# Three rotating score banks, moved maxima and a pipelined FFN in a pre-norm attention and FP8 FFN kernel

## The chip, the cores and the metric

The kernel runs on one core of one Trainium2 chip. The metric is the device time of the whole launch in microseconds (us); lower is better. Engines are named as the profile names them: PE is TensorE (matmuls), PEld its weight loads, DVE is VectorE, ACT is ScalarE, POOL is GpSimd, and SP is the queue that issues most DMAs.

## The reference

The input x has 2 batches of 2048 tokens of 512 values. A layer norm, grouped-query attention with 16 query heads and 2 key heads of 32 values, and a residual come first. A second layer norm, an FP8 matmul with one scale for all of x and one for the weight, and a second residual follow.

```python
def _L0_attn_ref(x, wq, bq, wk, bk, wv, bv, wo, bo):
    q = (x @ wq + bq).reshape(b, s, H, hd)          # H = 16, hd = 32
    k = (x @ wk + bk).reshape(b, s, G, hd)          # G = 2
    v = (x @ wv + bv).reshape(b, s, G, hd)
    ...
    q = q * cos + rotate_half(q) * sin
    q = q * hd ** (-0.5)
    k = k * cos + rotate_half(k) * sin
    ...
    scores = jnp.einsum('bqhd,bkhd->bhqk', q, k_exp) * hd ** (-0.5)
    attn = jax.nn.softmax(scores, axis=-1)
    out = jnp.einsum('bhqk,bkhd->bqhd', attn, v_exp).reshape(b, s, d)
    return out @ wo + bo

def _L0_ffn_ref(x, weight):
    w_fp8, w_scale = _quant_e4m3(weight)            # scale = max(|t|) / 448
    x_fp8, x_scale = _quant_e4m3(x2d)               # one scale for all of x
    out2d = _scaled_mm(x_fp8, w_fp8.T, x_scale, w_scale)
    return out2d.reshape(*x.shape[:-1], out2d.shape[-1])
...
x = x + _L0_attn_ref(_layernorm(x, axis=-1), ...)
x = x + _L0_ffn_ref(_layernorm(x, axis=-1), L0_ffn_weight)
```

## The kernel before

Tokens are cut into 8 blocks of 512 (`NBLK`), four to a batch; a block has 4 tiles of 128 rows. Queries are cut into 4 quads of 4 heads, and each quad of a block into 2 halves of 256 queries. One quad half is a unit; there are 64, in order.

**Scores twice.** The softmax needs each row's largest score before the exponential. `scores_for_maxima` computes the scores of the next unit with queries on the partitions: 32 matmuls of 128x512 (L457), each into one PSUM bank of the pool `ps_s`, each reduced by DVE (L464) into `part`. The pool has two banks. They come in pairs: two matmuls and two reductions, then a `yield`. At the end of a unit's scores DVE takes the largest over the key blocks (`mx`, L471), casts it into the first half of `mrow` (L472), and subtracts it to get the second half, the rest that the cast lost (L473). `gather_maxima` transposes `mrow` on PE into one more `ps_s` bank (`mtp`, L484), and ACT copies it out as `mT` (L488). The main pass computes the scores with keys on the partitions: `probabilities` lets PE subtract the maxima (L826, first two chunks only) and accumulate the scores (L835) in one of two double banks `T`, and ACT takes the exponential (L844) into `p`. POOL adds pairs of `p` (L818), DMAs add some of these sums to others (L886, L888), and `columns` multiplies p with the values (L795) and sums with ones (L806), both into the bank `avs`. `finish_heads` copies `avs` out on ACT (L774), takes reciprocals on DVE (L778) and multiplies on POOL (L779).

**The order of the work.** It is written out by hand (`manual_schedule`); each engine runs its own instructions in that order. A unit has 4 rounds of 4 key chunks. A round is: one pair of scores, two T chunks and their exponentials, a pair, in the last round `gather_maxima`, a `fill` on PE (not in round 0), the third T chunk, a pair, the fourth chunk, a `fill` on PE, a pair, two `fill`s on DVE, and `columns`. A unit's last pair of scores stands in round 2 of the unit before it.

**Side work.** Projections, norms and finishing are generators, which `Job` wraps. Each `yield` names the engine that its next piece needs (`ON_PE`, `ON_DVE`, `OTHER`), and `fill` runs one piece of the first job that is able to and due (`job.due <= step[0]`; a step is a round). `queue` holds the jobs that use a projection bank, and only its first job runs: the key and value projection of a block four ahead (`project_kv`), the query projection of the next block (`project_q`), the output projection (`finish_block`), the FFN weight (`prepare_weight`). `beside` holds jobs without such a bank: `stack_keys` (keys and their differences to the keys 256 earlier, `dk`, are split into two halves by ACT and POOL and stored to DRAM), `turn` (rotary embedding of queries) and `second_norm`. In the main loop all projections use one PSUM bank of the pool `ps_work`, through `bank`. Each evacuates it on ACT (`pq`, `pk`, `tp`, `tv`, `wtp`) or on DVE (`po`).

**Norms.** `layernorm_stats` makes mean and variance on DVE and lets POOL take the power that gives `rstd` (L190). `second_norm` then normalizes each tile into a scratch (L524) and takes its largest absolute value (L533), which is all that it is for: the common scale of x for the FFN.

**FFN.** After all units, for each half of a block (2 tiles): ACT scales x (L924), DVE rounds it to FP8 values in four instructions (`round_e4m3`, L210 to L216), PE transposes each tile (L936), ACT copies it (L938), PE multiplies (L941), ACT scales the product (L945), DVE adds the residual (L946), and SP stores the half (L948). Here the order is not written by hand.

Of the kernel before, what the change touches and what calls it, by code (L numbers as in the profile page):

```python
# [16 lines left out]
P = 128  # L17
# [10 lines left out]
def preln_attn_fp8_ffn_kernel(  # L28
# [54 lines left out]
    ON_PE, ON_DVE, OTHER = "PE", "DVE", "other"  # L83
    BACK = HB
# [12 lines left out]
    ps_s = ctx.enter_context(tc.tile_pool(name="ps_s", bufs=2, space=bass.MemoryType.PSUM))  # L97
    ps_av = ctx.enter_context(tc.tile_pool(name="ps_av", bufs=1, space=bass.MemoryType.PSUM))
    ps_work = ctx.enter_context(tc.tile_pool(name="ps_work", bufs=1, space=bass.MemoryType.PSUM))
# [4 lines left out]
    spread = [0]  # L104

    def bank(name, dtype=F32):

        shape = [P, TB * 4 // mybir.dt.size(dtype)] if dtype != F32 else [P, TB]
        if attending[0]:
            return ps_work.tile(shape, dtype, tag="work", name=name)  # L110
        if name[:2] in ("pk", "pq"):
            pool, tag = (ps_av, "av") if name[1] == "k" else (ps_work, "work")
            return pool.tile(shape, dtype, tag=tag, name=name)
        spread[0] += 1
        return ps_t.tile(shape, dtype, tag="EO"[spread[0] % 2], name=name)

# [61 lines left out]
    def layernorm_stats(src, mean, rstd, name, tiles=range(NT)):  # L178
# [11 lines left out]
        nc.gpsimd.tensor_tensor(rstd[:, at], var[:, at], neg_half[:, at], ALU.pow)  # L190

    def quantized_scale(amax, scale, inv, name):
# [4 lines left out]
        nc.vector.tensor_reduce(whole, across[:1, :P], AX.X, ALU.max)  # L197
        down = bank(f"down_{name}")

        nc.tensor.matmul(down[:, :1], sel[:1, 0, :].bitcast(F32), whole, start=True, stop=True)  # L200
        nc.vector.tensor_scalar(scale, down[:, :1], -1.0 / E4M3_MAX, 1e-12, ALU.mult, ALU.max)
        nc.vector.reciprocal(inv, scale)
# [27 lines left out]
    def normalized(n, xt, xnT, name):  # L230
# [17 lines left out]
        for i in range(0, NT, 2):  # L248
# [4 lines left out]
            for h in (i, i + 1):  # L253
# [8 lines left out]
                )  # L262

# [77 lines left out]
    def project_kv(n, xt, xnT, csb):  # L341
# [14 lines left out]
        nc.scalar.activation(kv, pk, AF.Identity, bias=bkv_sb)  # L356
        if attending[0]:
            u = swapped(kv, KD, f"k_{n}")
        else:
            u = yield from rotated(kv, csb, f"k_{n}")  # L360
# [7 lines left out]
        )  # L368
        if attending[0]:
# [4 lines left out]
    def stack_keys(n, kv, u, csb):  # L374
# [6 lines left out]
        for what in ("kS", "dkS"):  # L381
# [3 lines left out]
            else:  # L385
                src = t2(f"dk_{n}")[:KD]
                nc.gpsimd.tensor_tensor(src, kx[:, BACK:], kx[:, :TB], ALU.subtract)
            far = halves_far[what, b]
# [13 lines left out]
    def project_q(n, xnT, csb):  # L402
        q = wide.tile([P, QUADS, TB], F32, tag="q", name=f"q_{n}", bufs=2)
        for m in range(QUADS):
# [5 lines left out]
            nc.scalar.activation(raw, pq, AF.Identity, bias=bq_sb[:, m : m + 1])  # L410
            if attending[0]:
# [34 lines left out]

    def scores_for_maxima():

        for u, (k, half) in enumerate(units):
# [3 lines left out]
            for i, kb in order if u else sorted(order, key=lambda at: at[1]):  # L453
                for j in range(4):
                    s = ps_s.tile([P, TB], F32, tag="s", name=f"s_{u}_{i}_{kb}_{j}")
# [9 lines left out]
                    if j == 1:  # L465
                        yield u
                if (i, kb) == (HT - 1, NKB - 1):
# [4 lines left out]
                    nc.vector.tensor_copy(mview[:, :, :, 0], mx)  # L472
                    nc.vector.tensor_tensor(  # L473
                        mview[:, :, :, 1], mx, mview[:, :, :, 0].bitcast(F32), ALU.subtract
                    )
# [4 lines left out]
    def gather_maxima(u):  # L480

        tp = ps_s.tile([P, TB], F32, tag="s", name=f"mtp_{u}")
# [21 lines left out]
    def add_output(n, xt, attn, i, dims=range(DC)):  # L504
# [9 lines left out]
        nc.vector.tensor_tensor(xt[:, i, :], po, xt[:, i, :], ALU.add)  # L514

    def second_norm(n, xt, tiles=range(NT)):
# [3 lines left out]
        )  # L520
        for i in tiles:
            yield ON_DVE
            t = t2(f"xn2_{n}_{i}")
            nc.vector.tensor_scalar(  # L524
                t,
                xt[:, i, :],
                mean2[:, n, i : i + 1],
                rstd2[:, n, i : i + 1],
                ALU.subtract,
                ALU.mult,  # L530
            )
            yield ON_DVE
            nc.vector.tensor_reduce(  # L533
                amax2[:, n * NT + i : n * NT + i + 1], t, AX.X, ALU.max, apply_absolute_value=True
            )
# [39 lines left out]
    def prepare_weight(w_all):  # L575
# [8 lines left out]
        nc.vector.tensor_reduce(wmax1, wmax, AX.X, ALU.max)  # L584
        inv = const.tile([P, 1], F32, tag="winv", name="winv")
        quantized_scale(wmax1, w_scale, inv, "w")
        for o in range(DC):
# [6 lines left out]
            tp = ps_work.tile([P, DC, P], BF16, tag="work", name=f"wtp_{o}")  # L594
            for c in range(DC):
                nc.tensor.transpose(tp[:, c, :], w[o][:, c * P : (c + 1) * P], ident_bf)
            nc.scalar.copy(wT[:, :, o * P : (o + 1) * P], tp)

# [59 lines left out]
    class Job:  # L658


        def __init__(self, steps, kind=None, due=0):
            self.steps = steps
            self.due = due
            self.kind = kind or next(steps)

        def step(self):
            self.kind = next(self.steps, None)

# [48 lines left out]
    def enqueue(u):  # L717
# [20 lines left out]
        if n > 0 and n - 1 not in x_asked and soon:  # L738
# [177 lines left out]
    for n in range(NBLK):  # L916
        yt = y_near[n]
        for half in range(NT // 2):
            v = ppool.tile([P, 2, D], F32, tag="p", name=f"v8_{n}_{half}")
            magic = ppool.tile([P, 2, D], F32, tag="p", name=f"magic_{n}_{half}")  # L920
            xq = papool.tile([P, 2, D], BF16, tag="pa", name=f"xq_{n}_{half}")
            for h in range(2):
                i = 2 * half + h
                nc.scalar.activation(  # L924
                    v[:, h, :],
                    yt[:, i, :],
                    AF.Identity,
                    bias=plus[:, n, i : i + 1],
                    scale=times[:, n, i : i + 1],
                )  # L930
            run(round_e4m3(xq, v, magic))
            for h in range(2):
                i = 2 * half + h
                tp = ps_s.tile([P, DC, P], BF16, tag="s", name=f"xtp_{n}_{i}")
                for c in range(DC):
                    nc.tensor.transpose(tp[:, c, :], xq[:, h, c * P : (c + 1) * P], ident_bf)  # L936
# [66 lines left out]
```

## Time and profile before

| What | Value |
|---|---|
| median of 3 runs | 2551.72 us (2551.22 to 2552.48) |
| the profiled execution's own time | 2555.82 us |
| its span, first to last instruction | 2554.0 us |
| mean granted PE clock | 0.944 |
| prologue, to the first L826 | 123 us |
| main loop, to the last L774 | 2297 us |
| last output projection, scale, and FFN | 134 us |
| busy: PE, DVE, POOL, ACT | 2292.0, 1824.7, 1573.9, 1196.8 us |

Busy time is a sum over the span; what bounds a stage is read from which wait ends last there. A wait in the profile is the idle time of one engine, put down to what released it. Ends of matmuls are modelled, so distances between starts say more about PE than its busy time does. Line numbers (L457) are those of the kernel before.

### The profile page before, as it was taken

What the parts mean: (1) busy time and instruction counts of PE and PEld (TensorE: products, weight loads), DVE (VectorE), ACT (ScalarE), POOL (GpSimd) and SP (SyncE); (2) the same over time, 40 slices, a digit from 0 to 9 for tenths busy, and PEclk for the clock granted to TensorE, in tenths of its full rate; (3) what the DMA queues carried; (4) which work ended last, traced back from release to release, by engine and by line L of the source; (5) the groups of instructions that cost most, each with busy time, mean ns of one, the idle gap of its engine ahead of it and who ended that gap; (6) DMA issues with size and microseconds to landing.
All of it is one profiled execution on the core that took longest, in us unless ns stands there. A gap on an engine that the chain in (4) does not pass through costs nothing.

```text
span 2554.0 us, 41075 instructions
## 1 busy us (share of the span) xinstructions
PE 2292.0 (90%) x16514; PEld 1301.2 (51%) x16514; DVE 1824.7 (71%) x2836; ACT 1196.8 (47%) x1381; POOL 1573.9 (62%) x975
## 2 busy tenths in 40 slices
PE   5599999999999999999999989998998898989855
PEld 2255555555555555555555545555554554555422
DVE  3577677767786678767777687777777778777476
ACT  2145445544445444544444445544554444445444
POOL 4267676776667667666657666665675666656700
PEclk9699999999999999999999999999999999999956
DMA  7544554544444446354564444543454344544312
GB/s 225 147 83 94 111 121 99 118 112 87 120 104 116 90 88 149 94 131 93 116 142 91 108 106 94 115 83 86 111 104 98 75 106 109 130 103 99 67 50 83
DMA packets 103263, 271.71 MB, mean 106 GB/s; under 512 B 15776, under 2 KB 16416, under 8 KB 99232
## 3 DMA queue, kind: packets, MB, share of 16 engines
q0 software_dynamic: 36864, 134.23, 27.7%
q1 hardware_dynamic: 63792, 133.47, 17.7%
q8 instruction: 129, 2.11, 0.3%
q10 hardware_dynamic: 2416, 1.38, 0.2%
q14 instruction: 62, 0.51, 0.1%
HBM read 83.43 MB, written 42.99 MB: 49 GB/s over the span
## 4 chain that ended last, share of the span: by engine, by line
PE 54%; DVE 29%; POOL 5%; issue 3%; DMA 3%; ACT 3%; SPq 1%; DVEq 0%; POOLq 0%; ACTq 0%
DVE part L464 19%; PE s L457 14%; PE T L835 11%; PE avs L795 9%; PE avs L806 5%; PE po L268 4%; PE pq L268 3%; POOL pa L818 3%; DVE both L778 2%; PE T L826 2%; PE py L941 2%; DVE mrow L472 2%; ACT p L844 1%; PE mtp L484 1%; DVE sw_q L286 1%
## 5 line engine op out<-in xcount | busy, mean ns | idle before, releaser
L464 DVE TENSOR_REDUCE part<-s 128x1 f32<-128x512 f32 x2048 | 1316.1, 685 | 593.9 <-PE s L457 584.1
L818 POOL TENSOR_TENSOR pa<-p,p 128x1024 f32<-128x1024 f32 x448 | 1078.1, 2411 | 497.1 <-ACT p L844 486.2
L844 ACT ACTIVATE p<-T 128x1024 f32<-128x1024 f32 x1024 | 1004.4, 1023 | 807.3 <-PE T L835 789.4
L457 PE MATMUL s<-kS,qst 128*128 128x512 f32 x2048 | 882.8, 483 | 137.8 <-DVE part L464 79.2
L835 PE MATMUL T<-qst,dkS 128*128 128x512 f32 x2048 | 685.9, 432 | 16.1 <-ACT p L844 15.9
L457 PEld LDWEIGHTS s<-kS,qst 128*128 128x128 f32 x2048 | 376.0, 193 | 591.3 <-DVE part L464 417.3
L795 PE MATMUL avs<-p,vX 128*32 128x256 f32 x8192 | 498.9, 384 | 0.0
L835 PEld LDWEIGHTS T<-qst,dkS 128*128 128x128 f32 x2048 | 376.4, 194 | 159.7 <-issue 53.9
L795 PEld LDWEIGHTS avs<-p,vX 128*32 128x32 f32 x8192 | 240.8, 110 | 216.5 <-issue 71.1
L886 POOL DMA_DIRECT2D pa<-pa x192 | 170.1, 886 | 60.9 <-POOL pa L818 58.3
L774 ACT COPY both<-avs 128x512 f32<-128x512 f32 x64 | 37.5, 586 | 253.1 <-PE avs L806 253.1
L223 POOL TENSOR_TENSOR lo_q<-q,hi_q 128x512 fp32r<-128x512 f32 x32 | 41.1, 1284 | 178.4 <-ACT hi_q L222 178.1
L268 PE MATMUL po<-wo_sb,attn 128*128 128x512 f32 x256 | 135.0, 613 | 3.4 <-POOL attn L779 3.4
L268 PE MATMUL pq<-xnT_q,wq_sb 128*128 128x512 f32 x224 | 117.8, 608 | 0.0
L778 DVE RECIPROCAL both<-both 128x128 f32<-128x128 f32 x128 | 112.5, 920 | 6.5 <-ACT both L774 6.5
L806 PE MATMUL avs<-pa,ones 128*32 128x256 f32 x1536 | 106.3, 379 | 3.1 <-POOL pa L818 2.0
L941 PE MATMUL py<-wT,xqT 128*128 128x512 bf16 x128 | 56.6, 593 | 35.3 <-ACT xqT L938 35.3
L826 PEld LDWEIGHTS T<-mT,sel 128*128 128x128 f32 x512 | 78.8, 190 | 11.9 <-issue 0.4
L888 POOL DMA_DIRECT2D pa<-pa x64 | 75.7, 1183 | 11.7 <-DMA pa<-pa 10.2
L826 PE MATMUL T<-mT,sel 128*128 128x256 f32 x512 | 81.7, 282 | 0.0
L472 DVE CAST mrow<-mx 128x8 fp32r<-128x8 f32 x64 | 76.3, 1192 | 2.2
L779 POOL TENSOR_TENSOR attn<-both 128x256 f32<-128x256 f32 x64 | 65.7, 1026 | 6.0 <-DVE both L778 6.0
(115 smaller groups left out, 1212.9 us busy)
## 6 DMA issues: line engine op xcount, KB each, us to landing
pa<-pa POOLq DMA_DIRECT2D x256, 512.0 KB, 4.7
qst<-q_far SPq DMA_DIRECT2D x128, 256.0 KB, 4.2
x_kv<-in_L_attn_x_dram SPq DMA_DIRECT2D x8, 1024.0 KB, 8.0
q_far<-hi_q SPq DMA_DIRECT2D x32, 256.0 KB, 2.0
q_far<-lo_q SPq DMA_DIRECT2D x32, 256.0 KB, 2.0
x_res<-in_L_attn_x_dram SPq DMA_DIRECT2D x8, 1024.0 KB, 6.3
out_dram<-v SPq DMA_DIRECT2D x16, 512.0 KB, 2.8
sw_q<-q SPq DMA_DIRECT2D x240, 32.0 KB, 2.2
```

The lines of the kernel that those rows point to most:

```text
L268: nc.tensor.matmul(dst, lhs(c), rhs(c), start=(c == 0), stop=(c == chunks - 1))
L457: nc.tensor.matmul(s, qst[k][:, j, at : at + P], stacked["kS"][:, group(k), kb * TB : (kb + 1) * TB], start=True, stop=True,)
L464: nc.vector.tensor_reduce(part[:, i, j, kb : kb + 1], s, AX.X, ALU.max)
L472: nc.vector.tensor_copy(mview[:, :, :, 0], mx)
L778: nc.vector.reciprocal(piece, piece)
L795: nc.tensor.matmul(avs[j * HD : (j + 1) * HD, 0, :], vX[batch(k)][:, kc, group(k), :], p[:, j, :], start=(kc == 0), stop=(kc == NTS - 1), ...
L806: nc.tensor.matmul(avs[j * HD : (j + 1) * HD, 1, :], ones, pa[:, j, :], start=False, stop=(chunks[-1] == NTS - 1 and i == len(sums) - 1), ...
L818: nc.gpsimd.tensor_tensor(pa, a, b, ALU.add)
L826: nc.tensor.matmul(T[:, j, :], sel[:, j, :], maxima[u], start=(j % 2 == 0), stop=True, skip_group_check=True,)
L835: nc.tensor.matmul(T[:, j : j + 2, :], stacked["dkS"][:, group(k), kc * P : (kc + 1) * P], qst[k][:, j : j + 2, half * HB : (half + 1) * H ...
L844: nc.scalar.activation(p, T, AF.Exp, scale=SCALE)
L886: nc.gpsimd.dma_start(out=far_sums[r], in_=pair, accum_op=ALU.add)
```

## The change

Six edits go together.

1. The pool `ps_s` gets three banks by name (s0, s1, s2) and `ps_work` is gone. Scores take the three in turn (`s_bank`). A projection takes the one that is next in turn (`bank` sets `lent`), scores then alternate between the other two, and `give_back`, called where the evacuation has been issued, ends the loan.
2. The first half of the maxima is copied by ACT. The subtraction is put off until the next two reductions have been issued (`split_maxima`), or until `gather_maxima`.
3. A new mark `LATER` makes a job due one round later. It stands after POOL's `rstd`, before the halves of keys and of `dk` are split, and before the weight's scale is made.
4. `second_norm` takes the largest and the smallest value of each raw row (two reductions a tile) and normalizes these two at the end with four small instructions and a reduction, where it normalized the whole tile.
5. Loading x for the residual waits, in most cases, until a buffer of x is free.
6. The FFN is ordered by hand: rounding is issued two halves ahead, a tile's transpose one tile ahead of its product. The rounding's scratch moves to another buffer.

```diff
+    S_BANKS = 3
+    s_next = [0]
+    lent = [S_BANKS - 1]
+    def s_bank():
+        if s_next[0] == lent[0]:
+            s_next[0] = (s_next[0] + 1) % S_BANKS
+        tag = f"s{s_next[0]}"
+        s_next[0] = (s_next[0] + 1) % S_BANKS
+        return tag
     def bank(name, dtype=F32):
...
         if attending[0]:
-            return ps_work.tile(shape, dtype, tag="work", name=name)
+            if lent[0] is None:
+                lent[0] = s_next[0]
+            return ps_s.tile(shape, dtype, tag=f"s{lent[0]}", name=name)
...
+    def give_back():
+        if attending[0]:
+            lent[0] = None
...
         nc.gpsimd.tensor_tensor(rstd[:, at], var[:, at], neg_half[:, at], ALU.pow)
+        if attending[0]:
+            yield LATER
...
             raw = q[:, m, :]
             nc.scalar.activation(raw, pq, AF.Identity, bias=bq_sb[:, m : m + 1])
+            give_back()
...
                 nc.gpsimd.tensor_tensor(src, kx[:, BACK:], kx[:, :TB], ALU.subtract)
+            if attending[0]:
+                yield LATER
+                yield OTHER
             far = halves_far[what, b]
...
+    def split_maxima():
+        if split:
+            mview, mx = split.pop()
+            nc.vector.tensor_tensor(
+                mview[:, :, :, 1], mx, mview[:, :, :, 0].bitcast(F32), ALU.subtract
+            )
...
-                    s = ps_s.tile([P, TB], F32, tag="s", name=f"s_{u}_{i}_{kb}_{j}")
+                    s = ps_s.tile([P, TB], F32, tag=s_bank(), name=f"s_{u}_{i}_{kb}_{j}")
...
                     if j == 1:
+                        split_maxima()
                         yield u
...
                     nc.vector.tensor_reduce(mx, part, AX.X, ALU.max)
-                    nc.vector.tensor_copy(mview[:, :, :, 0], mx)
-                    nc.vector.tensor_tensor(
-                        mview[:, :, :, 1], mx, mview[:, :, :, 0].bitcast(F32), ALU.subtract
-                    )
+                    nc.scalar.copy(mview[:, :, :, 0], mx)
+                    split.append((mview, mx))
...
+        ends = small.tile([P, NT, 2], F32, tag="ends", name=f"ends_{n}_{tiles[0]}")
         for i in tiles:
-            yield ON_DVE
-            t = t2(f"xn2_{n}_{i}")
-            nc.vector.tensor_scalar(t, xt[:, i, :], mean2[...], rstd2[...], ALU.subtract, ALU.mult)
-            yield ON_DVE
-            nc.vector.tensor_reduce(amax2[...], t, AX.X, ALU.max, apply_absolute_value=True)
+            for e, op in enumerate((ALU.max, ALU.min)):
+                yield ON_DVE
+                nc.vector.tensor_reduce(ends[:, i, e : e + 1], xt[:, i, :], AX.X, op)
+        at = slice(tiles[0], tiles[-1] + 1)
+        yield ON_DVE
+        for e in range(2):
+            end = ends[:, at, e]
+            nc.vector.tensor_tensor(end, end, mean2[:, n, at], ALU.subtract)
+            nc.vector.tensor_tensor(end, end, rstd2[:, n, at], ALU.mult)
+        nc.vector.tensor_reduce(amax2[...], ends[:, at, :], AX.X, ALU.max, apply_absolute_value=True)
...
         nc.vector.tensor_reduce(wmax1, wmax, AX.X, ALU.max)
+        yield LATER
+        yield ON_PE
         inv = const.tile([P, 1], F32, tag="winv", name="winv")
         quantized_scale(wmax1, w_scale, inv, "w")
...
         def step(self):
             self.kind = next(self.steps, None)
+            if self.kind == LATER:
+                self.due = step[0] + 1
+                self.kind = next(self.steps)
...
-        if n > 0 and n - 1 not in x_asked and soon:
+        free = len(x_taken) < 3 or x_taken[-3] in x_done
+        if n > 0 and n - 1 not in x_asked and soon and (free or len(queue) <= 1):
...
-    for n in range(NBLK):
-        yt = y_near[n]
-        for half in range(NT // 2):
...
+    with tc.manual_schedule():
+        tiles = [(n, i) for n in range(NBLK) for i in range(NT)]
+        AHEAD = 4
+        for n, i in tiles[:AHEAD:2]:
+            round_half(n, i // 2)
+        ready = transposed(0, 0)
+        for at, (n, i) in enumerate(tiles):
+            if i % 2 == 0 and at + AHEAD < len(tiles):
+                m, j = tiles[at + AHEAD]
+                round_half(m, j // 2)
+            ahead = transposed(*tiles[at + 1]) if at + 1 < len(tiles) else None
+            multiplied(n, i, ready)
+            ready = ahead
```

`round_half`, `transposed` and `multiplied` hold the instructions of the FFN's loop body as they were: scaling and rounding of a half; the transposes of a tile with ScalarE's copy; the product, its scaling, the residual and, after a half's second tile, the store.

## The prediction

> **What bounds the kernel now.** I read the page's busy shares and clock row first, then its chain and groups, then the list of waits, then the timeline at the longest holes of TensorE, and windows over units and stages.
>
> ```profile
> PE 2292.0 (90%) x16514; PEld 1301.2 (51%) x16514; DVE 1824.7 (71%) x2836; ACT 1196.8 (47%) x1381; POOL 1573.9 (62%) x975
> PE 54%; DVE 29%; POOL 5%; issue 3%; DMA 3%; ACT 3%; SPq 1%; DVEq 0%; POOLq 0%; ACTq 0%
> L464 DVE TENSOR_REDUCE part<-s 128x1 f32<-128x512 f32 x2048 | 1316.1, 685 | 593.9 <-PE s L457 584.1
> L472 DVE CAST mrow<-mx 128x8 fp32r<-128x8 f32 x64 | 76.3, 1192 | 2.2
> ```
>
> ```profile
> PEld s L457 <- DVE part L464: 417.3, 933, 6.2
> ...
> ACT hi_dkS L222 <- POOL dk L387: 42.3, 8, 7.5
> ...
> DVE xn L524 <- POOL rstd L190: 16.1, 9, 5.1
> ```
>
> TensorE looks 90% busy, but those ends are modelled, so I took starts. Score matmuls follow each other in 0.22 us when nothing holds them. Counting the main stretch (123 to 2420 us) in start-to-start distances, 1788 us is streaming and 508 us is waiting: about 8 us in each of 64 units of 35.5 us (a unit ends where L774 copies `avs`). Half of it stands before a score matmul `s`: there are two score banks, and a pair may only start when VectorE's maximum has freed each. The chain says so too: 29% of it is VectorE, mostly L464.
>
> The worst recurring wait is at the end of each unit's scores:
>
> ```profile
> 1554.18 4.72 POOL L818 TENSOR_TENSOR pa<-p,p 128x1024 f32<-128x1024 f32 x2 [1.14 <-ACT p L844]
> ...
> 1556.84 0.19 DVE L471 TENSOR_REDUCE mx<-part 128x8 f32<-128x32 f32 x1
> 1557.07 1.88 DVE L472 CAST mrow<-mx 128x8 fp32r<-128x8 f32 x1
> ...
> 1558.98 0.17 DVE L473 TENSOR_TENSOR mrow<-mx,mrow 128x8 fp32r<-128x8 f32 x1
> 1559.07 2.56 DVE L464 TENSOR_REDUCE part<-s 128x1 f32<-128x512 f32 x4
> ...
> 1559.80 0.19 PEld L457 LDWEIGHTS s<-kS,qst 128*128 128x128 f32 x1 [0.70 <-DVE part L464]
> ```
>
> An 8-column cast (175 ns at its shortest) takes 1.88 us and ends as POOL's sum ends (1554.18 + 4.72 = 1558.90). The reductions behind it start late, and the scores behind them.
>
> ```profile
> 1488.29 1.68 POOL L190 TENSOR_TENSOR rstd<-var,neg_half 128x4 f32<-128x4 f32 x1
> ...
> 1490.01 2.57 DVE L524 TENSOR_SCALAR xn<-x_res,mean,rstd 128x512 f32<-128x512 f32 x1 [1.76 <-POOL rstd L190]
> 1492.51 1.28 DVE L464 TENSOR_REDUCE part<-s 128x1 f32<-128x512 f32 x2
> 1493.23 0.29 PEld L457 LDWEIGHTS s<-kS,qst 128*128 128x128 f32 x1 [6.20 <-DVE part L464]
> ```
>
> Here VectorE stands on `rstd`, then on the same coupling, and TensorE stands 6 us.
>
> ```profile
> 682.00:688.50 6.50, 4.56 (x41) 2.36 (x40) 6.33 (x12) 2.30 (x3) 3.93 (x3) 1.00 0.99 303
> 688.50:692.00 3.50, 3.31 (x10) 2.44 (x9) 2.03 (x4) 1.40 (x2) 1.50 (x2) 0.51 1.04 222
> ...
> 1464.10:1502.80 38.70, 32.24 (x243) 18.43 (x244) 30.61 (x48) 16.86 (x19) 21.87 (x13) 0.91 0.32 66
> 1536.20:1568.20 32.00, 30.83 (x243) 17.20 (x244) 24.35 (x37) 16.73 (x18) 20.89 (x12) 1.00 0.35 66
> ...
> 2435.40:2554.00 118.60, 70.90 (x256) 27.21 (x256) 81.63 (x96) 60.16 (x96) 0.00 (x0) 0.56 0.19 71
> ```
>
> Columns: length, busy PE, PEld, DVE, ACT, POOL, granted clock. Two things: after a hole the clock falls to half, and in the FFN no engine is full (DVE 81.6 of 118.6).
>
> **The change part by part**, against the profiled span of 2554.0 us. That execution took 2555.82; the runs' median is 2551.72, so I take the sum off the median.
>
> *Maxima on ScalarE.* From the timeline of 62 units, the score pair before `mtp` waits 1.21 us on average, any other pair 0.06. Without four units held by `rstd` (next part) it is 0.90. The cast leaves VectorE and the subtraction L473 goes behind the next two reductions, so of about 1.8 us ahead of these (0.19, 1.19, 0.44) only `mx` (0.19) stays: 62 x (0.90 - 0.06), about 52, take 50. On ScalarE the copy is new; L774 (512 columns, 0.586) and L488 (256, 0.373) give an estimate of 0.17 us, 11 us in all, and before the next exponential ScalarE stands 2.95 us for TensorE at 1559.17. Behind it in ScalarE's queue stand the exponentials, and TensorE's T behind those: if `mx` came over 2 us late they would wait. VectorE can be three reductions late (1.9 us), so cost 0, bound 64 x 0.5 = 32.
>
> *POOL's results a round later.* `dk` holds ScalarE, so the exponentials, so T: holes of 4.08 us at 287, 533, 826 and 1119 us, 3.2 each: 13. `rstd` of the second norm: holes of 6.1 at 1493, 1773, 2135, 2279, less the 1.2 just counted: 19. The weight's largest: one of 4.9 at 1943: 4. `rstd` for keys: 3. Together 39. The two `lo` sums, `dk` and four stores a block move: in the order of instructions the `dkS_far` stores of blocks 5 to 7 go behind eight `sw_q` transfers on SP's queue, `lo_kS` and `dk` behind sums on POOL's. The key fetch reads them, from 1141.7 us on for block 7, and 16 `sw_q` transfers stand behind it on SP. SP waits 961 us at L437 alone, which covers these 0.45 us issues; cost 0, bound 10 once where the stores come late. The guard on loading x changes nothing: both orders force the same four advances.
>
> *Row ends.* Out: 32 L524 (1.105 mean, 0.544 median) = 35.4. In: 32 more reductions like L533 (0.679) = 21.7, and five small operations per block. The Trainium skill speaks against these: GPSIMD Engine Reference, 1. Specifications, says that GpSimd shares its SBUF interfaces with VectorE and contends with instructions in a two-port mode or with two SBUF inputs. Four of the five have two. If each block's group waits a whole sum (2.4), 9 blocks cost 22 us. The trace's nearest row is L473, two small inputs: median 0.176, mean 0.441, longest 2.31. I take that row: 9 x (4 x 0.441 + 0.2) = 18. VectorE gets +4, in units where it is the long one (30.6 of 38.7): -4; bounds +10 and -15.
>
> *Third bank.* Where no projection holds a bank, three rotate. By the changed order 799 of 2071 score and `mtp` tiles of the main loop find three. At just these places TensorE now waits 187 us, of which 39 is counted above: 148. Not all can go. Following one undisturbed round of unit 39 by hand (pairs when the bank freed three tiles ago is free, T when its exponential ends, VectorE 0.645 a reduction), I get 0.9 us less a round, as the third pair meets VectorE's pace; 97 such rounds give 87. But 14 of these 24 units carry norm work on VectorE. I take 58; ends 0 and 110.
>
> *Hand-overs.* A bank given back is often the very next score's. In the changed order 105 score matmuls wait on ScalarE, before 63 (these for `mT`): 42 new ones, behind `pq` (21), `tp`, `tv`, `wtp`. A score directly behind the last `pq` waits for the exponential ahead and L410 (0.68): up to 1.15 us. A VectorE wait would often stand there anyway: I take 0.5 each, -21; ends 0 and -48. The 14 behind `po` come after the 1.9 us of avs: nothing.
>
> *The clock.* 25 stretches in the main loop run at half clock, 116 us. The Trainium skill's TensorE: Matmul & The Clock Gate (HAM oscillation) lets the clock fall for idle gaps over about 3.4 us; by that only the nine holes over 4 us matter, and the maxima's would cost no clock. The trace differs: at 688.5 the clock is halved right after a hole of 2.2 us, at 1016 after 2.5, at 617 after 1.5. So I count the 18 stretches that follow holes removed here, 92 us; less 24 us idle, half is 34 at most. Units also wait on other engines: 17; by the rule 8.
>
> *FFN.* VectorE's own work is 16 x (0.694 + 0.693 + 1.225 + 1.220) + 32 x 0.692 = 83.4. With rounding two halves ahead it need not stand for L945. First inputs 1.6, the last tiles' TensorE and ScalarE 5, the last store 4 as now, 4 of remaining stalls: 98 against 118.6. TensorE at half clock needs 2.4 a tile, 77, just under it. Gain 20; ends 8 (tiles at 3.1 as now) and 26.
>
> Sum: 50 + 39 - 4 + 58 - 21 + 17 + 20 = 159. 2551.7 - 159 = 2393 us.
>
> **The rivals.** *The third bank comes to nothing* (0.20): waits move from banks to ScalarE's exponentials and the DMA sums. For it: rounds are already 7.0 us at 1472 to 1479, with T just behind the exponential; the last `pa` accumulate is issued at 1559.80, lands 4.7 us later, and its columns need it at 1567.09. Against: in that round three pairs still wait. Then 101 remain, with hand-overs at their worst 74: 2450 to 2478.
>
> *Free units reach their floor* (0.13): third bank 110, clock 34: 2551.7 - 228 = 2324, up to 2345. VectorE's 30.6 us in norm units speaks against.
>
> *Hand-overs decide* (0.05, slower): a projection and the scores now share banks on TensorE's one in-order queue. There are 93 loans and 42 returns behind ScalarE. If each stands for three queued reductions (1.94 us), 262 us are lost against 180 gained elsewhere: 2634. It turns the sign from 1.33 us each. Against: each product takes its bank at least one fill before its first matmul, and 23 loans take back the same bank.
>
> **How the numbers follow.** About 0.2% is what a measurement here tells from no change. Main case 0.61 (2345 to 2445), third bank to nothing 0.20, floor 0.13, hand-overs 0.05, a near-cancelling 0.01. Likeliest 2393; 2328 to 2465 leaves out two in ten, at both sides. Faster 0.94, same 0.01, slower 0.05.
>
> **What would show it.** Right: the mrow copy is ScalarE's at about 0.2 us and the pair before `mtp` waits under 0.3; no T hole behind `dk`, no 6 us hole behind `rstd`; half-clock stretches fall to under ten; units 39, 47 and 61 (32.0 now) take 28 to 29.5, units with projections stay near 34; the FFN takes 95 to 102. Wrong: `s` <- ACT waits above 50 us; units 39 and 47 over 31; `avs` <- DMA or POOL growing from 8 to over 40 us; ScalarE standing on `mx`.

## The result, and the profile after

The changed kernel takes 2513.69 us (median of 4 runs, 2507.04 to 2517.14), the kernel before 2551.47 beside it: ratio 0.9849, interval [0.9827, 0.9871]. That is 38 us less. The forecast was 159 less, and its range ended at 2465. The profiled execution took 2512.17 us, with a span of 2510.1. From here on, a line number in a run's view is that of the run's own kernel: the reduction of the scores is L464 before and L502 after.

The page of the changed kernel: busy time of each engine, the chain's shares, the costliest group.

```profile
PE 2220.7 (88%) x16509; PEld 1286.6 (51%) x16514; DVE 1766.0 (70%) x2817; ACT 1207.4 (48%) x1445; POOL 1571.5 (63%) x975
...
PE 38%; DVE 22%; POOL 15%; DMA 11%; issue 7%; ACT 5%; SPq 1%; POOLq 0%; ACTq 0%; DVEq 0%
...
L502 DVE TENSOR_REDUCE part<-s 128x1 f32<-128x512 f32 x2048 | 1299.6, 682 | 643.6 <-PE s L495 637.9
```

TensorE and VectorE have lost weight in the chain (54 to 38%, 29 to 22%), as meant. POOL has gone from 5 to 15% and DMA from 3 to 11%. The forecast had no term for either.

The list of waits (who waits for whom: us in all, times, longest) shows what fell and what came:

```profile
PEld s L495 <- DVE part L502: 264.1, 675, 5.5
PE mtp L522 <- DVE part L502: 54.2, 39, 4.7
PEld avs L859 <- DMA pa<-pa: 40.2, 30, 3.0
PEld s L495 <- ACT q L437: 32.3, 23, 1.7
PE avs L859 <- DMA pa<-pa: 25.7, 28, 2.5
```

The same waits before, for `mtp` and for the ones-matmuls on the DMA:

```profile
PE mtp L484 <- DVE part L464: 11.9, 58, 0.3
PEld avs L806 <- DMA pa<-pa: 2.6, 4, 1.3
PE avs L806 <- DMA pa<-pa: 1.2, 2, 0.8
```

(One wait can stand in two rows, once for the weight load, PEld, and once for the matmul, PE.) The wait for score banks fell from 417 to 264 us. In its place TensorE stands before `mtp`, before the ones-matmuls that sum the probabilities (L859), and, as new waits, behind `pq`'s evacuation.

TensorE's waiting in the main loop, counted as in the prediction (distance from start to start, less the streaming time of the matmul before), is the table all runs are read with. The loop runs here from the first selection matmul to the last copy of `avs`. A pair of scores has a first and a second matmul.

| us of TensorE waiting before | before | after |
|---|---|---|
| first score of the pair ahead of `mtp` | 74.7 | 2.6 |
| other first scores | 93.2 | 78.4 |
| first scores behind an evacuation | -32.3 | 2.9 |
| second scores | 216.5 | 180.9 |
| T | 87.6 | 72.2 |
| `mtp` | 34.0 | 77.1 |
| ones-matmuls | 1.1 | 42.6 |
| everything else | 30.1 | 24.4 |
| all | 504.9 | 481.1 |

(The negative entry only means that the streaming time used for a product, 0.436 us, is too long where a score follows it; differences count.) Scores, the first four rows, had 352 of the 505 us before, more than the half of which the prediction speaks. About 144 us went and 120 came back. The loop's 24 us and the FFN's 26 (118.6 to 92.3) less some 6 us of a longer prologue make the difference of 44 between the spans. The prologue took 123 to 131 us in the runs of this study, also where no edit touches it.

The largest thing that came back is seen in the timeline of unit 35. It took 35.2 us before and 40.4 after (columns: start, us, engine, line, operation):

```profile
1427.22 1.20 POOL L941 DMA_DIRECT2D pa<-pa  x1
1427.46 4.58 DVE L481 TENSOR_TENSOR mrow<-mx,mrow 128x8 fp32r<-128x8 f32 x1
...
1427.79 1.91 POOL L540 TENSOR_TENSOR x_res<-x_res,bo_sb 128x512 f32<-128x512 f32 x1
1429.03 2.97 POOL L871 TENSOR_TENSOR pa<-p,p 128x1024 f32<-128x1024 f32 x1
1431.96 1.27 DVE L502 TENSOR_REDUCE part<-s 128x1 f32<-128x512 f32 x2
...
1432.79 0.66 PE L522 MATMUL mtp<-ident,mrow 128*128 128x128 f32 x2 [4.68 <-DVE part L502]
```

L481 is the subtraction that the change puts off. It has eight columns and a median of 0.165 us. Here it takes 4.58 and ends as the second of two adjoining POOL sums does (1429.03 + 2.97 = 1432.00, the subtraction at 1432.04). The reductions behind it wait, and `mtp` with them. `mtp` has such holes of 4.9 to 5.0 us in units 14, 22, 30, 35, 43, 53 and 57, and these units are each 5 to 6.5 us longer than before. Units 37, 45, 55 and 59, which waited for `rstd`, became 7 to 9 us shorter.

The groups by tile give the same over all 64 units (shortest, median, longest in ns). Cast and subtraction before:

```profile
L472 DVE CAST mrow<-mx x64: 175/1332/2127, 114.6 to 2380.2; 128x8 fp32r<-128x8 f32 x64
L473 DVE TENSOR_TENSOR mrow<-mx,mrow x64: 174/176/2312, 114.8 to 2381.2; 128x8 fp32r<-128x8 f32 x64
```

and after:

```profile
L511 ACT CAST mrow<-mx x64: 203/205/210, 119.6 to 2362.5; 128x8 fp32r<-128x8 f32 x64
L481 DVE TENSOR_TENSOR mrow<-mx,mrow x64: 154/165/4579, 120.8 to 2362.9; 128x8 fp32r<-128x8 f32 x64
```

In the trace of before, 53 of the 64 casts L472 last over 0.3 us, and every one of the 53 ends 0.03 to 0.04 us behind the end of a POOL instruction. Of the subtractions L481 after, 23 are that long, and again all 23 end so; 10 of these lasted through two POOL operations. So the subtraction meets POOL less often than the cast did, but for longer, and at a place where `mtp` needs it next.

The FFN, in the table by windows (length, then busy PE, PEld, DVE, ACT, POOL, clock):

```profile
2417.80:2510.10 92.30, 52.06 (x251) 23.27 (x256) 80.35 (x101) 59.88 (x96) 0.00 (x0) 0.78 0.24 91
```

VectorE is busy for 80 of 92 us, so here the edit did what it says, and a little more than forecast. (This window opens 0.8 us ahead of the first scaling of x, with which the window before opens; from the first scaling it is 91.4 us.)

### The profile page after: what moved, and what is told of

It is laid out like the page before. It is cut to its first block, busy times and chain, and to the rows that moved or that the text cites. A ratio compares the mean times of both kernels' runs of the same rounds, so it can differ in the third digit from the quotient of the medians.

```text
span 2510.1 us, 41080 instructions
## 1 busy us (share of the span) xinstructions
PE 2220.7 (88%) x16509; PEld 1286.6 (51%) x16514; DVE 1766.0 (70%) x2817; ACT 1207.4 (48%) x1445; POOL 1571.5 (63%) x975
## 3 DMA queue, kind: packets, MB, share of 16 engines
q1 hardware_dynamic: 63792, 133.47, 18.1%
## 4 chain that ended last, share of the span: by engine, by line
PE 38%; DVE 22%; POOL 15%; DMA 11%; issue 7%; ACT 5%; SPq 1%; POOLq 0%; ACTq 0%; DVEq 0%
DVE part L502 12%; POOL pa L871 11%; PE s L495 10%; DMA pa<-pa 9%; PE T L888 7%; PE avs L848 7%; ACT p L897 4%; PE po L290 4%; PE avs L859 3%; DVE both L831 3%; PE pq L290 2%; PE T L879 2%; DVE mrow L481 2%; POOL pa L939 1%; POOL q L324 1%
## 5 line engine op out<-in xcount | busy, mean ns | idle before, releaser
L502 DVE TENSOR_REDUCE part<-s 128x1 f32<-128x512 f32 x2048 | 1299.6, 682 | 643.6 <-PE s L495 637.9
L495 PE MATMUL s<-kS,qst 128*128 128x512 f32 x2048 | 828.5, 466 | 101.3 <-DVE part L502 29.5
L495 PEld LDWEIGHTS s<-kS,qst 128*128 128x128 f32 x2048 | 367.9, 191 | 497.2 <-DVE part L502 264.1
L888 PEld LDWEIGHTS T<-qst,dkS 128*128 128x128 f32 x2048 | 369.8, 191 | 157.0 <-issue 53.7
L939 POOL DMA_DIRECT2D pa<-pa x192 | 169.1, 881 | 60.9 <-POOL pa L871 58.3
L290 PE MATMUL po<-wo_sb,attn 128*128 128x512 f32 x256 | 140.1, 634 | 3.4 <-POOL attn L832 3.4
L859 PE MATMUL avs<-pa,ones 128*32 128x256 f32 x1536 | 107.7, 383 | 36.5 <-DMA pa<-pa 25.7
L859 PEld LDWEIGHTS avs<-pa,ones 128*32 128x32 f32 x1536 | 46.3, 110 | 80.9 <-DMA pa<-pa 40.2
L522 PE MATMUL mtp<-ident,mrow 128*128 128x128 f32 x128 | 29.0, 311 | 61.0 <-DVE part L502 54.2
L941 POOL DMA_DIRECT2D pa<-pa x64 | 74.8, 1168 | 11.8 <-DMA pa<-pa 10.2
```

What stands on the lines that cost most here:

```text
L290: nc.tensor.matmul(dst, lhs(c), rhs(c), start=(c == 0), stop=(c == chunks - 1))
L495: nc.tensor.matmul(s, qst[k][:, j, at : at + P], stacked["kS"][:, group(k), kb * TB : (kb + 1) * TB], start=True, stop=True,)
L502: nc.vector.tensor_reduce(part[:, i, j, kb : kb + 1], s, AX.X, ALU.max)
L859: nc.tensor.matmul(avs[j * HD : (j + 1) * HD, 1, :], ones, pa[:, j, :], start=False, stop=(chunks[-1] == NTS - 1 and i == len(sums) - 1), ...
L888: nc.tensor.matmul(T[:, j : j + 2, :], stacked["dkS"][:, group(k), kc * P : (kc + 1) * P], qst[k][:, j : j + 2, half * HB : (half + 1) * H ...
L939: nc.gpsimd.dma_start(out=far_sums[r], in_=pair, accum_op=ALU.add)
```

## The experiments

Three theories were tried against each other. *Port*: the put-off subtraction waits for POOL. *Hand-overs*: the third bank's gain is lost where scores take over a bank that ScalarE must still empty. *Sums*: the sum that POOL's DMA accumulates lands too late for the ones-matmuls.

| run | what | us | ratio to before |
|---|---|---|---|
| after | all edits | 2513.7 | 0.9849 [0.9827, 0.9871] |
| a_split_now | after, subtraction at once | 2492.5 | 0.9761 [0.9729, 0.9794] |
| a_keep_bank | after, banks handed back to projections | 2503.5 | 0.9799 [0.9761, 0.9837] |
| a_no_third | after, scores on two banks | 2504.9 | 0.9808 [0.9771, 0.9845] |
| a_no_lo | after, no subtraction | 2463.6 | 0.9645 [0.9624, 0.9666] |
| a_no_lo_two | the last two together | 2445.2 | 0.9579 [0.9564, 0.9595] |
| a_old_max | after without edit 2 | 2495.5 | 0.9773 [0.9749, 0.9797] |
| a_old_norm | after without edit 4 | 2522.1 | 0.9866 [0.9851, 0.9881] |
| a_near | after, first sum on TensorE | 2446.0 | 0.9567 [0.9549, 0.9585] |
| b_max | before with edit 2 | 2585.9 | 1.0141 [1.0114, 1.0168] |
| b_direct | before, neither cast nor subtraction | 2515.8 | 0.9845 [0.9827, 0.9863] |
| b_later | before with edit 3 | 2541.1 | 0.9956 [0.9938, 0.9975] |
| b_later_guard | before with edits 3 and 5 | 2526.7 | 0.9888 [0.9868, 0.9908] |
| b_ffn | before with edit 6 | 2530.1 | 0.9898 [0.9860, 0.9936] |
| best1 | two banks, no subtraction, first sum on TensorE | 2439.0 | 0.9543 [0.9522, 0.9564] |
| best2 | best1 with the third bank | 2434.4 | 0.9522 [0.9504, 0.9541] |
| best3 | best2 with banks handed back | 2418.3 | 0.9461 [0.9444, 0.9479] |

The kernel before measured between 2551 and 2555 us in the groups of runs, so the ratios are what is compared below; 0.001 is 2.55 us.

**The subtraction at once.** In a_split_now it stands right behind ScalarE's copy.

```diff
                     split.append((mview, mx))
+                    split_maxima()
```

> The changed kernel (2513.7 us), with the subtraction L481 directly behind ScalarE's copy, not behind the next two reductions. Theory 'port' (L481 has two SBUF inputs and now falls where POOL issues its two sums back to back, up to 4.6 us; mtp waits 77 us where it waited 34): at the old place POOL is at the end of one sum, so L481's mean falls from 0.87 to under 0.5 us, mtp's wait to about 35, and the time by 30 to 45 us, to 2470 to 2484. Theory 'hand-overs' or theory 'sums' (other waits hold TensorE anyway): 2500 to 2515, the wait only moves.

Faster than the changed kernel by about 22 us, less than the port theory asked for. The groups by tile of this run tell why:

```profile
L511 ACT CAST mrow<-mx x64: 203/205/208, 117.2 to 2343.3; 128x8 fp32r<-128x8 f32 x64
L481 DVE TENSOR_TENSOR mrow<-mx,mrow x64: 165/1194/2362, 118.5 to 2343.6; 128x8 fp32r<-128x8 f32 x64
```

The median of the subtraction is now 1.19 us. In before the cast had 1.33 and the subtraction behind it 0.18. So moving the cast to ScalarE does not remove the wait: the subtraction inherits it (57 of 64 wait, each to the end of a POOL sum), while the reduction `mx` ahead of it stays at 0.19 us. Before `mtp` 43.6 us of waiting went, but 48 came back on the scores around it. The run's gain shows in the sums' wait, 42.6 to 24.5, and in small items.

**Edit 2 alone.** b_max is the kernel before with nothing but this edit; its two parts are as in the diff above.

> The kernel before with edit 2 alone (copy on ScalarE, subtraction behind the next two reductions). As forecast: 50 us and a few of clock, 2495 to 2502. If the subtraction takes over the wait for POOL that the cast had (port): what is saved ahead of the two reductions is lost in front of mtp, 2535 to 2555.

It is slower than before, by 1.4%, outside both expectations. The groups by tile of b_max:

```profile
L483 ACT CAST mrow<-mx x64: 203/205/208, 121.4 to 2420.6; 128x8 fp32r<-128x8 f32 x64
L453 DVE TENSOR_TENSOR mrow<-mx,mrow x64: 157/165/4560, 121.6 to 2421.1; 128x8 fp32r<-128x8 f32 x64
```

The pair ahead of `mtp` waits 36 us instead of 75, as the edit intends. `mtp` itself waits 85 instead of 34, and the ones-matmuls 17 instead of 1. T, which stands behind the copy in ScalarE's queue, waits only some 4 us longer.

**Edit 2 taken out.** a_old_max makes both halves on VectorE, at once, in the changed kernel.

```diff
-                    nc.scalar.copy(mview[:, :, :, 0], mx)
+                    nc.vector.tensor_copy(mview[:, :, :, 0], mx)
                     split.append((mview, mx))
+                    split_maxima()
```

> The changed kernel without edit 2: VectorE makes both halves of the maxima at once, as before. If edit 2 is a loss in place as it is alone (port, 34 us alone): 2475 to 2500. If it is needed in the changed order, as forecast: slower than the changed kernel, 2535 to 2565.

0.9773 against 0.9849: in place, too, edit 2 costs some 19 us. a_old_max and a_split_now differ only in the engine of the first half, and their intervals overlap (0.9773 and 0.9761). So the copy's move to ScalarE is worth next to nothing, and what costs is that the subtraction is put off.

**No subtraction.** a_no_lo copies the first halves on ScalarE and stops there.

```diff
                     nc.scalar.copy(mview[:, :, :, 0], mx)
-                    split.append((mview, mx))
```

> The changed kernel without the subtraction L481: the second halves of the maxima stay zero, which a softmax does not see but for rounding. Port theory: the wait before mtp falls from 77 us to about 30 and the reductions behind are on time, 45 to 60 us less: 2454 to 2469. If the DMA sums and hand-overs hold the units anyway (sums): 10 to 20 us less, 2494 to 2504.

52 us less (0.9645 against 0.9849), as the port theory said. `mtp` waits 33.2 us instead of 77.1. The ones-matmuls still wait 52.6.

**What there was to be had.** b_direct reduces the maximum straight into `mrow` in the kernel before.

```diff
-                    nc.vector.tensor_reduce(mx, part, AX.X, ALU.max)
-                    nc.vector.tensor_copy(mview[:, :, :, 0], mx)
-                    nc.vector.tensor_tensor(
-                        mview[:, :, :, 1], mx, mview[:, :, :, 0].bitcast(F32), ALU.subtract
-                    )
+                    nc.vector.tensor_reduce(mview[:, :, :, 0], part, AX.X, ALU.max)
```

> The kernel before with one change: the maximum is reduced straight into mrow, so that neither copy nor subtraction is there (the second halves stay zero). Port theory: all of the 0.84 us that the pair before mtp waits over other pairs goes, and part of the 34 us at mtp: 55 to 80 us less, 2472 to 2497. Rival, that the next wait takes its place: 2520 to 2540.

40 us less, between the two expectations. The pair ahead of `mtp` went from 74.7 to 36.2 only. Some 24 of the 36 stand in units 37, 45, 55 and 59, 5.9 us in each, behind `xn`, which waits for `rstd`: they belong to edit 3. The ones-matmuls came up to 14. So of the forecast 50, this way brings some 40 in the kernel before. No operation is left in it that waits for POOL: the reduction into `mrow` takes 0.19 us in all 64 units (0.191 at the longest).

**The third bank taken out.** In a_no_third the loan never ends, so projections keep the third bank as in the kernel before. a_no_lo_two does the same without the subtraction.

```diff
     def give_back():
-        if attending[0]:
-            lent[0] = None
+        return
```

> The changed kernel with the third bank always lent: scores use two banks and projections the third, as before the change; all other edits stay. If the third bank is worth what the forecast had for it net of hand-overs (37 us): 2551. If hand-overs and the sums eat it: 2500 to 2520. If it costs more than it brings: below 2500.

> As a_no_lo, and projections keep the third bank, so that scores have two. If the third bank is worth what was forecast once the subtraction is out of the way: 35 to 58 us slower than a_no_lo. If it gives and takes alike, as in a_no_third: within 10 us of a_no_lo.

Without the subtraction, two banks are faster than three: 0.9579 against 0.9645. With it the difference is 10 us the same way, 0.9808 against 0.9849, but the intervals overlap a little. The waits tell what it gives and takes. From a_no_third to after, first and second scores lose 48 us of waiting and `mtp` 4; scores behind an evacuation gain 35, the ones-matmuls 21, T 4.

**Banks handed back.** a_keep_bank lets a projection take the bank that the last one gave back, if no score was placed in between.

```diff
     def s_bank():
+        back[0] = None
...
-                lent[0] = s_next[0]
+                lent[0] = s_next[0] if back[0] is None else back[0]
...
     def give_back():
         if attending[0]:
+            back[0] = lent[0]
             lent[0] = None
```

> The changed kernel, but a projection that goes on in the same step keeps the bank that it has just given back, so scores do not land on a bank that ScalarE still has to empty. Theory 'hand-overs' (scores behind an evacuation wait 35 us more than before the change): -20 to -35 us, 2479 to 2494. Theory 'port' or 'sums': within 8 us of 2513.7, with the wait of scores on ScalarE gone and found again elsewhere.

The scores behind an evacuation lose 10 of their 35 us, and the run is 13 us faster by the ratios, whose intervals overlap a little: between the two expectations. `mtp` still waits 73.2 us: the subtraction is a loss of its own.

**The sum on TensorE.** a_near does not let POOL's DMA add the first sum onto the second; four more matmuls a unit sum it in round 2, where it is there already.

```diff
-                    sums = []
+                    sums = [far_sums[0]] if r == 2 else []
                     far_sums.append(add_pair(u, chunks[2], *probs[2:]))
                     nc.gpsimd.dma_start(out=far_sums[r], in_=pair, accum_op=ALU.add)
-                if r == 2:
-                    nc.gpsimd.dma_start(out=far_sums[1], in_=far_sums[0], accum_op=ALU.add)
```

> The changed kernel without the DMA accumulate of the first sum onto the second: TensorE sums the first itself one round earlier. Sums theory: the 42.6 us that the ones matmuls wait go, less 14 us for 4 more matmuls a unit: 2480 to 2492. If the late subtraction ends the units anyway (port alone): 2508 to 2518.

72 us less (0.9567 against 0.9849), more than twice what the sums theory gave, although the expectation priced the added matmuls too low. Each counts twice in the trace: L859 has 2048 records where there were 1536, and a unit's eight more take 0.43 us from start to start, about 27 us in all and not 14. The ones-matmuls fall from 42.6 to 4.6, and `mtp` from 77.1 to 41.2. In the list of waits of a_near:

```profile
PE mtp L522 <- DVE part L502: 21.8, 40, 1.4
...
PEld avs L859 <- DMA pa<-pa: 0.4, 1, 0.4
```

The two losses hang together. Issuing the accumulate (L941) takes POOL 1.2 us, in the same place in each unit: between L939 and what follows. Without it POOL's queue is not in arrears when the subtraction comes. This is read from the rows: the run takes away the late sum, POOL's 1.2 us and the DMA's transfer at once, and none takes away one alone. The timeline of a_near at the place of unit 35 shown above:

```profile
1388.64 1.58 POOL L540 TENSOR_TENSOR x_res<-x_res,bo_sb 128x512 f32<-128x512 f32 x1
...
1389.30 0.96 DVE L481 TENSOR_TENSOR mrow<-mx,mrow 128x8 fp32r<-128x8 f32 x1
...
1390.88 2.37 POOL L871 TENSOR_TENSOR pa<-p,p 128x1024 f32<-128x1024 f32 x1 [0.66 <-ACT p L897]
```

POOL stands 0.66 us between the two sums, and the subtraction gets through in that gap after 0.96 us instead of 4.58. Over all units it now waits in 13 cases instead of 23, and through two POOL operations in 2 instead of 10.

**Pieces a round later.** b_later is before with the mark `LATER`; b_later_guard adds edit 5, the guard on loading x.

```diff
+        free = len(x_taken) < 3 or x_taken[-3] in x_done
-        if n > 0 and n - 1 not in x_asked and soon:
+        if n > 0 and n - 1 not in x_asked and soon and (free or len(queue) <= 1):
```

> The kernel before with edit 3 alone (pieces that need POOL a round later). As forecast: 39 us and some 10 of clock, 2502 to 2515. If the holes behind dk and rstd only give way to the next wait: under 15 us, 2537 to 2550.

> The kernel before with edits 3 and 5. If the 16 us hole of unit 19 in b_later came from an early load of x: it goes, and the forecast 39 us are seen, 2508 to 2522. If the guard has no part in it: as b_later, 2536 to 2548.

Edit 3 alone: 11 us. Unit 19 takes 53.9 us in it (41.6 before). There VectorE stands on the late transfer of query pieces, two waits of 18.1 us together. The row of b_later from 810 to 900 us, which has the longer one:

```profile
DVE sw_q L289 <- DMA sw_q<-q: 10.0, 1, 10.0
```

x is loaded at 822.5 us there, and the query pieces behind it on SP's queue go out from 832.0. With the guard x is loaded behind them (839.4), the unit takes 38.9, and the two edits are worth 29 us together. So the guard, which I had put at nothing, belongs to edit 3.

**The FFN and the row ends.** b_ffn is before with edit 6 alone; a_old_norm is after with the whole-tile `second_norm` of before.

> The kernel before (2551.5 us) with the new order of the FFN alone. The changed kernel's FFN took 92.3 us where 118.6 was: if that is the edit's own, 2523 to 2528; if half of it is the clock that the main loop hands over, about 2538.

> The changed kernel without edit 4: the second norm's largest comes from the whole normalized tile again. As forecast for the row ends (4 us gained): 2510 to 2520. If normalized tiles were waiting for POOL more than was counted: slower, 2525 to 2545.

The FFN's order is worth 26 us by the ratio (16 to 36 by its interval; 21 by the medians). The stage itself takes 91.0 us in the trace of b_ffn, as short as after, so its gain is the edit's own; in b_max and b_direct, with the old order, it takes 118.4 and 116.8. The row ends are worth 4, and their intervals overlap.

**The best of it.** best1 reduces straight into `mrow` as b_direct, keeps two banks for scores and sums on TensorE as a_near. best2 puts the third bank on it, best3 hands banks back as a_keep_bank.

> The changed kernel with the maximum reduced straight into mrow (no copy, no subtraction), two banks for scores, and no DMA accumulate of the first sum onto the second: TensorE sums the first itself one round earlier (4 more matmuls a unit). Sums theory: the 25 us of waits before the ones matmuls go, and POOL is 74 us less busy: 2405 to 2430. If other waits end last there: 2435 to 2450, as a_no_lo_two.

> best1 with the third bank shared as in the change. If the DMA sums were where the third bank's gain went: now it shows, 25 to 45 us faster than best1, 2394 to 2414. If the hand-overs eat it (35 us counted against 42 us): within 10 us of best1, 2429 to 2449.

> best2, and a projection takes again the bank that the last one gave back, if no score has been placed since. If hand-overs are the other half of the third bank's price: 10 to 25 us faster than best2. If not: within 5 us of it.

best3 is faster than both kernels: 2418.3 us, 0.9461. best1 came out at its second expectation, that other waits end last. Against after, no subtraction brought 52 us and the sum on TensorE 72, but both together (best2) 83: they are for the most part one loss. best1 to best2 is a test of the third bank with both other losses gone, and it gains only 5 us, with overlapping intervals, as the hand-overs theory had it. Scores wait 48 us less and `mtp` 9, those behind an evacuation 35 more, ones-matmuls 8 and T 7 more. best3 then gains 16, and the wait for `pq`'s evacuation, unchanged from after to best2, gives way:

```profile
PEld s L495 <- ACT q L437: 32.3, 23, 1.7
```

is best2's row, and best3's is

```profile
PEld s L498 <- ACT q L440: 13.8, 8, 1.7
```

The chain of best3 is TensorE's and VectorE's again, with POOL at 2% and DMA at 4:

```profile
PE 58%; DVE 27%; ACT 4%; DMA 4%; issue 3%; POOL 2%; SPq 1%; DVEq 0%; ACTq 0%; POOLq 0%
```

## Why the prediction was wrong

| step of the sum | forecast, us gained | measured, us gained |
|---|---|---|
| maxima on ScalarE | 50 | -19 in place, -36 alone |
| POOL's results a round later | 39 | 29 with the guard |
| row ends | -4 | 4 |
| third bank | 58 | 48 less of waits at scores |
| hand-overs | -21 | -35 |
| late sums | none | -21 with the third bank |
| clock | 17 | not measured by itself (half clock in the loop: 116 to 65 us) |
| FFN | 20 | 26 |

The third bank with what hangs on it is -10 in place (a_no_third, not clear of noise; -17 without the subtraction, which is). With -19, 29, 4 and 26 the single measurements add up to 30 us against the 38 of the whole.

*Maxima on ScalarE: the step that failed.* The prediction said that the subtraction "goes behind the next two reductions, so of about 1.8 us ahead of these only `mx` stays", and gave the moved instruction no cost at its new place. The pair's wait did go, 74.7 to 2.6 us. But at its new place the subtraction waits for POOL, in 23 of 64 units and for up to 4.58 us, and `mtp` behind it went from 34.0 to 77.1. The trace of before had shown the small cast waiting for POOL in 53 units. The row L473 had a median of 0.176 us only because it follows the cast, when POOL's sum has just ended; in 8 units it met the next sum and took 2.2 to 2.3 us. The prediction had these figures, a mean of 0.441 and a longest of 2.31, and used them for the row ends. It also named what the Trainium skill states (GPSIMD Engine Reference, 1. Specifications: POOL contends with VectorE instructions in a two-port mode or with two SBUF inputs), and applied it to the row ends alone. The subtraction has two SBUF inputs as well, so by the same statement it contends with POOL at its new place too; the 23 long ones agree.

*Row ends.* Here L473 served: the four small operations and the closing reduction were put at 18 us. In the profile after they take about 16.5: L571, first and third of each group of four, has 12.1 us for 18 instructions, L572 2.9 for 18. Where the group meets POOL, only its first instruction waits (up to 2.34 us at 1549.9); those behind it take 0.15 to 0.17. The edit brought 4 where -4 was forecast, inside its bounds and not clear of noise.

*Third bank and hand-overs.* 58 was 48 and 21 was 35: each within its bounds, both on the bad side. What the sum left out is in the first rival, "the third bank comes to nothing": faster rounds reach the DMA-accumulated sum before it has landed. It was given a chance of 0.20, with 101 us left in all. It came true for this edit, and of the listed signs, "`avs` <- DMA or POOL growing from 8 to over 40 us" was seen: weight loads alone waited 40 us on the DMA, and 14 on POOL. Weight loads of `s` waited 52 us for ScalarE (32 behind `q`, 11 behind `xnT_kv`, 9 behind `vX` and `wT`), just over the 50 named.

*POOL's results a round later.* The mechanism was right. T lost 17 us of waiting in b_later_guard (13 forecast), and units 37, 45, 55 and 59 lost 4.7 to 5.5 each (4.9 forecast). Missing are units 28 (39.5 to 44.4 us) and 51 (39.6 to 42.6), and 1 to 2 us in some units behind the shortened ones. Unit 28 is one in which keys are fetched. Their later stores alone are not its loss: b_later has them at the same distance, and unit 28 takes 39.1 there. What differs is x, which the guard loads 1.9 us ahead of the unit (33 us in b_later); the last of the fetched keys lands 25.6 us into the unit instead of 22.7. So the loss comes with the guard, which the prediction had put at nothing. Unit 51's stays open (39.8 in b_later).

*The signs.* Right as listed: the copy takes 0.205 us, the pair ahead of `mtp` waits 0.04 us, and the holes of 4.1 us behind `dk` and of 6.1 behind `rstd` are gone. ScalarE does stand on `mx`, a sign listed against the prediction (91.9 us in 64 waits), but in b_max T waits only some 4 us longer. Not reached: units 39 and 47 take 30.8 us (28 to 29.5 forecast, over 31 named as a sign against), unit 61 took 32.3 and did not fall, and half-clock stretches fell from 25 to 15, not below ten. After, too, they follow holes shorter than 3.4 us: half clock from 220.6 behind one of 1.8, and from 442.5 behind one of 2.2, so the prediction's reading of the trace holds. Even in best3, with none of the three losses at their full size, units 39, 47 and 61 take 30.3 to 30.4, so 29.5 was too low for them; units 38, 46 and 60 take 29.0 to 29.1 there.

*FFN.* 92.3 us against 95 to 102. VectorE's part was right (80.4 against 83.4 worked out). The stalls left over came out smaller. The granted clock in this stage rose from 0.56 to 0.78, and to 0.74 in b_ffn.

## What to carry to other kernels

An operation that waits for another engine need not lose its wait by being moved: before a small instruction is put off, ask what stands on the contended engine at the new place, and who is next in its queue; look at the longest of its kind, not the median. A cheap second instruction behind a waiting first is no measure of its own price. Where a stage is made faster, the next late thing may be an asynchronous accumulate nobody waited for so far: moving that sum to an engine with room (about 27 us of matmuls here), which also took its issue off the contended POOL, brought more than any edit of the change.

## What was unexpected of the hardware

The wait of the small cast and of the small subtraction on VectorE ends with a POOL operation, to within 0.05 us, in all 53 long casts of before and all 23 long subtractions of after; if POOL's next operation adjoins, it can last through that too (4.58 us for an operation of 0.165). The cast waits with one SBUF input, as the subtraction does with two. Reductions do not: L502 takes 0.682 us after and 0.694 at the longest, with 817 of its 2048 inside a POOL operation; L566, on an SBUF row, takes 0.675 and 0.680. Nor does the addition L552, with one operand in PSUM (0.682).

Not everything on POOL holds the subtraction. Of the 41 short ones after, 37 ran inside POOL's issuing of a DMA (L939 or L941, 0.9 to 1.2 us) and none inside a POOL sum. Seven of a_near ran in 0.16 us inside POOL's power for `rstd`, though that has two SBUF inputs:

```profile
425.40 1.35 POOL L207 TENSOR_TENSOR rstd<-var,neg_half 128x4 f32<-128x4 f32 x1
425.70 0.16 DVE L481 TENSOR_TENSOR mrow<-mx,mrow 128x8 fp32r<-128x8 f32 x1
```

The seven subtractions of 4.5 to 4.6 us after also began inside a DMA issue, 0.28 to 0.33 us ahead of the first sum's record. By the records they had time to end; why they did not stays open (times on POOL are rough).
